# Where attention's first inputs lie, how the relative terms are split, and in what order v and the output's inputs come

## The chip, the cores and the metric

The kernel runs on one core of one Trainium2 chip. The metric is the device time of one launch in microseconds (us); lower is better. The engines are called PE (matrix), DVE (vector), ACT (scalar), POOL and SP; here SP issues nearly all loads, POOL all stores. The chip's 16 DMA engines serve both.

## The reference

x has 48 x 48 = 2304 tokens of 768 channels in float32. Two layers each add a self-attention of the group-normalised x to x:

```python
for layer in (0, 1):
    h = group_norm(x, groups=32)
    q, k, v = split_heads(h @ qkv_w + qkv_b)      # 12 heads of 64; layer 0 adds low-rank terms to q and v
    rel_h = einsum('bhwc,hkc->bhwk', q, Rh)       # 48 values per token
    rel_w = einsum('bhwc,wkc->bhwk', q, Rw)       # 48 values per token
    a = softmax(q * scale @ k.T + rel_h[..., :, None] + rel_w[..., None, :])
    x = x + (a @ v) @ proj_w + proj_b
```

Scores are 2304 x 2304 for each head; rel_h and rel_w add a term by key row and one by key column.

## The kernel before, in words

Tokens are kept in 6 blocks of 384 along the free axis, with channels on partitions (xT). Heads go in 6 pairs of 128 channels. Per layer:

1. **Load and group norm** (L183, L201 on). x is transposed into xT; weights come through `Weights` (L255), which has two pools on the right side of SBUF, one for tables and biases, one double-buffered for weight matrices.
2. **project_kv** (L470). k and v by seven products in place of eight block products (`seven_products`, L425). k is stored to DRAM in a high and a low part (L557). v is computed in 9 iterations, each for two tiles of 128 tokens by 768 channels, and each tile is stored with one DMA from POOL (L584). v tiles alternate between two places.
3. **project_q** (L586). For each half (three pairs of heads) and block: PE makes ps_q (L673), DVE evicts it into x_q (L679), `store` (L613) splits it with `in_parts` (L376 to L386) into a high part, a cast by ACT, and a low part, a subtraction by DVE, in double-buffered part tiles, and stores each from POOL. ACT also copies x_q into `columns` (L684), reordered by image column. The table product psr gives rel_h by block (L632 to L646), straight from PSUM into parts. After the last block of a half, 96 table products psc (L620) in 16 groups of 96 x 432 give rel_w (L648 to L662): copies to a float32 tile relw, by turns on DVE (L658) and ACT (L660), whose writes stride through the tile; then `store` splits and stores relw in six blocks, 12 DMAs of 432 KB for each half.
4. **attend_plain** (L845 on). For a pair of heads and 512 queries, 18 key tiles: `scores` (L931 is the matmul helper) makes a 128 x 1024 score tile in eight matmuls of the q and k parts and two more of the `rel` tile with a 0/1 matrix; ACT takes the exponential (L957); DVE adds it to a sum (L963). `values` multiplies the exponentials with v, a batch of 6 tiles behind the scores. Matmuls are pinned in program order with `in_order` (L158). Inputs come in two sets, by turns: keys (L867, 6 DMAs for a pair), rel (L912, L916, 24 for 512 queries) and q (L902) from SP, v from POOL (L881), 24 DMAs for a pair, which put v's rows into the order of key tiles: a tile has 8 image rows by 16 columns. The two sets are pools on SBUF's left side, set 0 behind a ring of 13 exponential tiles, and set 1 behind it. Set 0's keys are over ground that is early free, its rel, q and v over weight tiles in use until the last ps_q. The output is stored by pair (L1006).
5. **out_project** (L1088). Three pairs of blocks, (0,3), (1,4), (2,5): the attention's output oT (L1082) and the residual (L1118) are loaded by SP, 21 products psy (L1130) a pair, seven for each of three groups of 128 channels, the sum and the next residual stored. `oT` and its helpers lie in left-side pools that start when attention's are free. `begin` (L1163) makes xT and the weights of the next layer; the main loop (L1175 to L1222) calls the stages in turn, and before out_project it issues layer 1's first weights (w_k, L346). `beside` loads the projection matrix (wproj) during attention.

A planner places instructions on each engine by estimated time, except those that `in_order` pins; the engines then run their own lists in order, and synchronise with semaphores. The kernel holds a second version of its attention ("shifted"), for inputs where the exponential could overflow; it is not executed with these inputs.

Of the kernel before, what the change touches and what calls it, by code (L numbers as in the profile page):

```python
# [9 lines left out]
F32 = mybir.dt.float32  # L10
# [8 lines left out]
P = 128  # L19
C = 768  # L20
CT = C // P
# [50 lines left out]
def compute(ctx: ExitStack, tc: tile.TileContext, x, layers, out, run, bad):  # L72
# [182 lines left out]
    class Weights:  # L255
# [7 lines left out]
        def __init__(self, es, ly, li):  # L263
            self.ly, self.li = ly, li
            self.loaded = {}
            self.one = es.enter_context(tc.tile_pool(name="p0_one", bufs=1, side="right", **REUSE))
            self.wp = es.enter_context(tc.tile_pool(name="p0_w", bufs=2, side="right", **REUSE))
            if ly.lora is not None:
                self.ps = es.enter_context(
                    tc.tile_pool(name="ps_f", bufs=2, space=PSUM, **REUSE)  # L270
                )
# [172 lines left out]
    def project(ly, li, xT, kv, weights, first, normalise):  # L444


        PARTS = range(1 if shifted else 2)
        PART = F32 if shifted else F32R
        qd, kd = (
            [[scratch(f"{x}{li}_{half}_{i}", [P, HP, N]) for i in PARTS] for half in range(2)]  # L450
            for x in "qk"
        )
        vd = scratch(f"v{li}", [N, C])
        rel_d = [
            [
                [scratch(f"r{li}_{a}_{half}_{i}", [2 * HG, HP, N]) for i in PARTS]
                for half in range(2)
            ]
            for a in range(2)
        ]  # L460
        project_kv(ly, li, xT, kv, weights, first, normalise, PARTS, PART, kd, vd)
        return qd, kd, vd, rel_d
# [7 lines left out]
    def project_kv(ly, li, xT, kv, weights, first, normalise, PARTS, PART, kd, vd):  # L470


        with ExitStack() as es:
# [28 lines left out]

                return sums, all_steps()

            def multiply(left, right, left_cols, right_cols, transposed, name):
                def product(i):
                    a, b = left[FACTORS[i][0]], right[FACTORS[i][1]]
                    ps = ps_mm.tile([P, QB], F32, tag="mm", name=f"ps_{name}_{i}")
                    for t in range(HP):
                        x, y = a[:, t, left_cols], b[:, t, right_cols]  # L510
                        nc.tensor.matmul(  # L511
                            ps, lhsT=y if transposed else x, rhs=x if transposed else y,
                            start=(t == 0), stop=(t == HP - 1),
                        )
                    return ps

                return product

            everything = slice(None)
            left, steps = first, ()  # L520
            for g in range(3):
                for _ in steps:
                    pass
                for b in range(HB):
# [4 lines left out]
                    def result(at, ps, more):  # L529
# [8 lines left out]
                        nc.vector.tensor_add(to, ps, more)  # L538

                    seven_products(kp, QB, multiply(  # L540
                        left, factors[b], everything, everything, False, f"k_{g}_{b}"
                    ), result)
                    for i in range(2):
                        pair = 2 * g + i
# [22 lines left out]
            for b in range(HB):  # L567
                if b == 1:
                    weights.fold(weights.take("q", 0)[0], 0, 0, ps_mm)
                for j in range(TPB):  # L570

                    place, tag = ((kv, "x"), (vp, "v"))[(b * TPB + j) % 2]
                    v = place.tile([P, 2, C], F32, tag=tag, name=f"v_{b}_{j}")

                    def result(at, ps, more):
                        i, k = int(at[0]) - 1, int(at[1]) - 1
                        nc.vector.tensor_add(v[:, k, ts(i, HP * P)], ps, more)  # L577

                    seven_products(kp, QB, multiply(
                        left, factors[b], everything, ts(j, P), True, f"v_{b}_{j}"  # L580
                    ), result)
                    for k in range(2):
                        at = (b + k * HB) * QB + j * P
                        nc.gpsimd.dma_start(vd[at : at + P, :], v[:, k])  # L584

    def project_q(ly, li, xT, weights, qd, rel_d):  # L586

# [3 lines left out]
        with ExitStack() as es:  # L591
# [55 lines left out]

            def rel_w(half, x):  # L648

                rel = one.tile([P, HP, N], F32, tag="rel", name=f"relw_{half}")[0 : 2 * HG]  # L650
                rel_of = rel.rearrange("p t (h w) -> p w t h", w=HG)
                for l0 in range(0, HG, 3):
                    ps = ps_rel.tile(
                        [2 * HG, 3, HP, HG], F32, tag="rel", name=f"psc_{half}_{l0}"
                    )
                    positions(1, ps, lambda l: x[:, :, l, :], l0, 3)
                    if l0 % 2:
                        nc.vector.tensor_copy(rel_of[:, l0 : l0 + 3], ps)  # L658
                    else:
                        nc.scalar.copy(rel_of[:, l0 : l0 + 3], ps)  # L660
                for b in range(NQB):
                    store(rel_d[1][half], b, rel[:, :, ts(b, QB)], f"relw_{half}_{b}")  # L662

            for half in range(2):
                w, _ = weights.take("q", half)
# [168 lines left out]
    def attend_plain(li, qd, kd, vd, rel_d, od, beside):  # L834
# [10 lines left out]
        ]  # L845
        with ExitStack() as es:

            pp = es.enter_context(tc.tile_pool(name="p2_p", bufs=2 * BATCH + 1, **REUSE))
            sets = [
                es.enter_context(tc.tile_pool(name=f"p2_in{i}", bufs=1, **REUSE)) for i in range(2)  # L850
            ]
            tp = es.enter_context(tc.tile_pool(name="p2_t", bufs=2, **REUSE))
            hp = es.enter_context(tc.tile_pool(name="p2_h", bufs=1, **REUSE))
            ps_s = es.enter_context(tc.tile_pool(name="ps_s", bufs=3, space=PSUM, **REUSE))
            ps_o = es.enter_context(tc.tile_pool(name="ps_o", bufs=1, space=PSUM, **REUSE))

# [16 lines left out]

            def fetch_values(pair):
                v = sets[pair % 2].tile([P, NKT, P], F32, tag="v", name=f"v{li}_{pair}")
                found = vd[:, ts(pair, P)].rearrange(
                    "(b i c w) d -> i w b c d", b=NQB, i=8, w=KG
                )
                for i in range(8):
                    for c in range(TPB):  # L880
                        nc.gpsimd.dma_start(  # L881
                            v.rearrange("p (b c) d -> p b c d", c=TPB)[ts(i, KG), :, c],
                            found[i, :, :, c],
                        )
                return v

            def fetch_queries(i, pair, at, n):
# [197 lines left out]
            )  # L1085
            lo += n

    def out_project(ly, li, od, w, bt, res, xT, next_res, beside):  # L1088


        last = xT is None
        with ExitStack() as es:
            rp = es.enter_context(tc.tile_pool(name="p3_r", bufs=2, **REUSE))
            tp = es.enter_context(tc.tile_pool(name="p3_t", bufs=1, **REUSE))
            kp = es.enter_context(tc.tile_pool(name="p3_k", bufs=2, **REUSE))
            yp = es.enter_context(tc.tile_pool(name="p3_y", bufs=2, **REUSE))
            ps_y = es.enter_context(tc.tile_pool(
                name="ps_y", bufs=4 if last else 8, space=PSUM, **REUSE
# [2 lines left out]
            if last:  # L1101
                op = es.enter_context(tc.tile_pool(name="p3_o", bufs=2 * TPB, **REUSE))
                ps_n = es.enter_context(tc.tile_pool(name="ps_n", bufs=2, space=PSUM, **REUSE))
            for b in range(HB):
                pair = (b, b + HB)
                if last and not shifted and b == HB - 1:
                    judge(ps_n)
                if last:
                    y = yp.tile([P, 2, CT, QB], F32, tag="y", name=f"y_{b}")
                    y = [y[:, i] for i in range(2)]  # L1110
                else:
                    y = [xT[:, i] for i in pair]
                oT = rp.tile([P, 2, CT, QB], F32, tag="oT", name=f"oT_{b}")
                for i in range(2):
                    fetch_output(oT[:, i], od, pair[i])

                for i in range(2):
                    nc.sync.dma_start(y[i], res[pair[i]])  # L1118
                blocks = {
                    f"{i + 1}{j + 1}": oT[:, j, i * HP : (i + 1) * HP]  # L1120
                    for i in range(2) for j in range(2)
                }
                t = tp.tile([P, 4, HP, QB], F32, tag="t", name=f"oT_t_{b}")
# [38 lines left out]
    residuals = [[scratch(f"res{li}_{b}", [P, CT, QB]) for b in range(NQB)] for li in range(2)]  # L1162
    def begin(li, es):  # L1163

        xp, gn = (
            es.enter_context(tc.tile_pool(name=f"{n}{li}", bufs=1, side="right", **REUSE))
            for n in ("x", "gn")
        )
        xT = xp.tile([P, NQB, CT, QB], F32, tag="xT", name=f"xT{li}")
        return xT, gn, Weights(es, layers[li], li)  # L1170

    es = ExitStack()
    xT, gn, weights = begin(0, es)
    for li, ly in enumerate(layers):
# [21 lines left out]
        with tc.tile_pool(name="p3_w", bufs=1, **REUSE) as p3:  # L1196
# [3 lines left out]
            w, steps = sums_of_a(matrix_blocks(w_all, HP * P), *(s[:, i] for i in range(3)))  # L1200

            def beside(w_all=w_all, bt=bt, steps=steps, ly=ly):
                nc.sync.dma_start(w_all, ly.proj_w.rearrange("(t p) n -> p t n", p=P))
                nc.sync.dma_start(bt, ly.proj_bt)
                yield
                yield from steps

            attend(li, qd, kd, vd, rel_d, od, beside())
            es = ExitStack()
            xT = None  # L1210
            if not last:
                xT, gn, weights = begin(1, es)
                weights.begin()
                weights.spread()
                weights.load(0)
                first, k_steps = third_of_k(weights, 0)
            out_project(
                ly, li, od, w, bt, residuals[li], xT,
                None if last else residuals[li + 1], () if last else k_steps,
            )  # L1220
    es.close()


# [53 lines left out]
```

## Time and profile before

| | us |
|---|---|
| median of 3 runs | 3395.48 |
| lowest, highest | 3394.51, 3401.37 |
| profiled execution | 3392.2 |
| its span on the core | 3390.5 |
| PE busy in the span | 3259.3 |
| exponentials L957, 1080 on ACT | 991.3 |

The span is what the hardware profiler saw from the first to the last instruction; the profiled execution's own time has 1.7 us more around it. Lines of groups give the busy time, the mean of one in ns, and after the second bar the engine's idle time just before them with what ended it. Lines of waits give the waiting engine and tile, the releaser, total us, times, longest us. In timelines, the first two numbers are start and length in us. PE's granted clock is given as a share of full speed; it was 0.981 over the span.

### The profile page before, as it was taken

The page shows a single profiled execution, that of the slowest core. Times are in us where ns is not written, and L with a number is a line of the kernel's source. Part 1 is how long each engine was busy: PE and PEld are TensorE (multiplying, and loading weights), DVE is VectorE, ACT ScalarE, POOL GpSimd, SP SyncE. Part 2 cuts the span into 40 slices and gives each one's busy share as a digit, 9 for nine tenths or more (in the row PEclk, how much of TensorE's full clock was granted, in tenths as well). Part 3 has the DMA queues.
Part 4 walks back from the last instruction along what each step waited for, and adds up shares of the span by engine and source line. Part 5 has one row for each costly group of instructions (what it writes and reads, how often), then busy time and mean ns, then how long its engine had stood idle before and what let it go on. Part 6 is the DMA issues. An engine that isn't in the chain of part 4 may idle for free. (4 is left out here: it accounts for less than half of the span.)

```text
span 3390.5 us, 50247 instructions
## 1 busy us (share of the span) xinstructions
PE 3259.3 (96%) x19708; PEld 2005.6 (59%) x19708; DVE 2111.9 (62%) x2267; ACT 1425.6 (42%) x1647; POOL 439.5 (13%) x795
## 2 busy tenths in 40 slices
PE   8999987999999999998989999699999999999997
PEld 5556664565656565655555566556565656566554
DVE  8533446777777676776674234467777677777753
ACT  3101445555555555552011024455555555555511
POOL 2101222020202020000011012400101020100000
PEclk9999998999999999999999999899999999999998
DMA  7322477353626262524233146654445352624051
GB/s 257 135 79 96 152 230 204 77 126 76 136 67 145 59 153 59 108 62 165 84 140 130 65 138 225 187 133 96 116 90 121 81 129 74 137 67 103 28 200 57
DMA packets 200723, 405.61 MB, mean 120 GB/s; under 512 B 42608, under 2 KB 82448, under 8 KB 197408
## 3 DMA queue, kind: packets, MB, share of 16 engines
q1 hardware_dynamic: 150816, 238.84, 28.7%
q0 software_dynamic: 49664, 163.47, 14.3%
q8 instruction: 159, 2.61, 0.3%
q14 instruction: 84, 0.69, 0.1%
HBM read 253.27 MB, written 148.89 MB: 119 GB/s over the span
## 5 line engine op out<-in xcount | busy, mean ns | idle before, releaser
L957 ACT ACTIVATE pt<-ps_sc 128x1024 f32<-128x1024 f32 (+1 forms) x1080 | 991.3, 939 | 663.1 <-PE ps_sc L931 595.8
L963 DVE TENSOR_TENSOR sum<-sum,pt 128x1024 f32<-128x1024 f32 (+1 forms) x960 | 1072.7, 1117 | 314.4 <-ACT pt L957 230.4
L931 PE MATMUL ps_sc<-q,k 64*128 64x512 f32 (+1 forms) x8640 | 1099.6, 374 | 59.0 <-ACT pt L957 58.4
L931 PEld LDWEIGHTS ps_sc<-q,k 64*128 64x128 f32 x8640 | 774.3, 186 | 326.8 <-issue 92.2
L931 PE MATMUL ps_ov<-pt,v 128*64 128x512 f32 (+1 forms) x4320 | 884.3, 554 | 0.0
L931 PEld LDWEIGHTS ps_ov<-pt,v 128*64 128x64 f32 x4320 | 293.5, 137 | 474.8 <-issue 432.9
L931 PE MATMUL ps_sc<-rel,places 64*128 64x512 f32 (+1 forms) x2160 | 410.9, 371 | 0.0
L673 PE MATMUL ps_q<-xT,w_q 128*128 128x384 f32 x864 | 285.8, 489 | 0.7 <-DVE v L577 0.7
L1008 POOL DMA_DIRECT2D f_rec<-rec x120 | 58.8, 495 | 1658.3 <-DVE rec L997 1609.5
L997 DVE RECIPROCAL rec<-ps_d 128x512 f32<-128x512 f32 (+1 forms) x60 | 182.2, 3037 | 100.7 <-PE ps_d L931 100.7
L673 PEld LDWEIGHTS ps_q<-xT,w_q 128*128 128x128 f32 x864 | 163.7, 192 | 111.2 <-issue 2.3
L931 PEld LDWEIGHTS ps_sc<-rel,places 64*128 64x128 f32 x2160 | 210.4, 185 | 29.7
L881 POOL DMA_DIRECT2D v<-f_v x288 | 148.7, 527 | 171.3 <-PE ps_ov L931 144.0
L511 PE MATMUL ps_k<-xt,w_k 128*128 128x384 f32 x432 | 143.4, 487 | 3.6 <-DVE xt L420 2.6
L679 DVE TENSOR_SCALAR x_q<-ps_q,bt 128x384 f32<-128x384 f32 x72 | 44.4, 616 | 137.5 <-PE ps_q L673 133.2
L511 PE MATMUL ps_k<-xT,w_k 128*128 128x384 f32 x324 | 115.6, 510 | 4.7 <-DVE xT L248 4.6
L511 PEld LDWEIGHTS ps_k<-xt,w_k 128*128 128x128 f32 x432 | 81.5, 190 | 63.0 <-PE ps_k L511 3.0
L972 ACT CAST sum<-sum 128x1024 bf16<-128x1024 f32 (+1 forms) x60 | 57.6, 961 | 129.0 <-DVE sum L963 129.0
L973 DVE TENSOR_TENSOR sum<-sum,sum 128x1024 f32<-128x1024 f32 (+1 forms) x60 | 67.1, 1119 | 61.6 <-ACT sum L972 61.6
L975 DVE TENSOR_TENSOR sum<-sum,sum 128x1024 bf16<-128x1024 f32 (+1 forms) x60 | 67.1, 1119 | 61.6 <-ACT sum L974 61.6
L381 ACT ACTIVATE xs_q<-x_q 128x1152 fp32r<-128x1152 f32 x24 | 27.9, 1164 | 181.1 <-DVE x_q L679 175.7
L963 DVE TENSOR_TENSOR sum<-pt 128x1024 f32<-128x1024 f32 (+1 forms) x60 | 67.1, 1118 | 56.9 <-ACT pt L957 55.8
(167 smaller groups left out, 2468.1 us busy)
## 6 DMA issues: line engine op xcount, KB each, us to landing
rel<-f_r SPq DMA_DIRECT2D x1152, 96.0 KB, 4.1
f_k<-xs POOLq DMA_DIRECT2D x72, 384.0 KB, 2.9
k<-f_k SPq DMA_DIRECT2D x72, 384.0 KB, 5.6
f_q<-xs_q POOLq DMA_DIRECT2D x48, 576.0 KB, 3.8
q<-f_q SPq DMA_DIRECT2D x96, 256.0 KB, 3.0
f_r<-relh POOLq DMA_DIRECT2D x48, 432.0 KB, 5.0
f_r<-relw POOLq DMA_DIRECT2D x48, 432.0 KB, 6.0
f_v<-v POOLq DMA_DIRECT2D x36, 384.0 KB, 2.6
```

The lines of the kernel that those rows point to most:

```text
L511: nc.tensor.matmul(ps, lhsT=y if transposed else x, rhs=x if transposed else y, start=(t == 0), stop=(t == HP - 1),)
L673: nc.tensor.matmul(ps, lhsT=w[:, t, ts(pr, P)], rhs=xT[:, b, t, :], start=(t == 0), stop=(t == CT - 1),)
L679: nc.vector.tensor_scalar(x[:, pr], ps, weights.bt[:, pair : pair + 1], ly.q_scale, ALU.add, ALU.mult,)
L881: nc.gpsimd.dma_start(v.rearrange("p (b c) d -> p b c d", c=TPB)[ts(i, KG), :, c], found[i, :, :, c],)
L931: in_order(nc.tensor.matmul(*args, **kwargs))
L957: nc.scalar.activation(pt, ps[:, :, 0 : self.n], AF.Exp)
L963: nc.vector.tensor_add(self.sum, self.first if kt == 1 else self.sum, pt)
L972: nc.scalar.copy(hi, self.sum)
L973: nc.vector.tensor_sub(self.sum, self.sum, hi)
L975: nc.vector.tensor_sub(lo, self.sum, mid)
L997: nc.vector.reciprocal(self.rec, ps)
L1008: nc.gpsimd.dma_start(recs[li][2 * self.pair + r : 2 * self.pair + r + 1, to], self.rec[r * HD : r * HD + 1, :],)
```

## The change

- **Rel terms.** `rel_w` no longer copies psc to a float32 tile. Each group goes with `in_parts` straight into two part tiles of the whole half: ACT casts the high part, DVE subtracts it from PSUM, both with the same strided writes. Each part is stored with one DMA for the half.
- **v's order.** Each v tile is stored with 16 DMAs of 16 rows, to the rows of DRAM where key tiles have them, and `fetch_values` is one DMA from SP for a pair.
- **Pools.** On the right side, the tables' pool is now outermost, then x, then the group norm's, then the weights' (a new method `room`). On the left, attention's pools are in the order set 1, rec and o, sum, exponential ring, set 0. The addresses of the built program show set 0 over what was xT (161,024 to 216,320 bytes of a partition), and v of set 0 partly over the tables; so keys and rel of set 0 wait for the last ps_q, and v for the last psc. Set 1 lies over the part tiles.
- **out_project.** The order of the pairs is (1,4), (0,3), (2,5). The first pair's oT goes into two blocks of the new xT (layer 0), or into a new pool on the right side (layer 1, also its residual); w_k of layer 1 is loaded after the first pair's loads. The projection matrix's two loads are pinned in program order.
- `multiply` is rewritten and gives the same matmuls.

```diff
@@ Weights
             self.one = es.enter_context(tc.tile_pool(name="p0_one", bufs=1, side="right", **REUSE))
+
+        def room(self, es):
             self.wp = es.enter_context(tc.tile_pool(name="p0_w", bufs=2, side="right", **REUSE))
@@ project_kv
                     for k in range(2):
-                        at = (b + k * HB) * QB + j * P
-                        nc.gpsimd.dma_start(vd[at : at + P, :], v[:, k])
+                        at = (b + k * HB) * QB
...
+                        for r in range(P // KG):
+                            i, c = divmod(8 * j + r, TPB)
+                            to = at + c * P + i * KG
+                            nc.gpsimd.dma_start(vd[to : to + KG, :], v[ts(r, KG), k])
@@ project_q, rel_w
-                rel = one.tile([P, HP, N], F32, tag="rel", name=f"relw_{half}")[0 : 2 * HG]
-                rel_of = rel.rearrange("p t (h w) -> p w t h", w=HG)
+                parts = [
+                    one.tile([P, HP, N], PART, tag=f"rel{i}", name=f"relw_{half}_{i}")[0 : 2 * HG]
+                    for i in PARTS
+                ]
                 for l0 in range(0, HG, 3):
...
-                    if l0 % 2:
-                        nc.vector.tensor_copy(rel_of[:, l0 : l0 + 3], ps)
+                    to = [
+                        r.rearrange("p t (h w) -> p w t h", w=HG)[:, l0 : l0 + 3] for r in parts
+                    ]
...
-                        nc.scalar.copy(rel_of[:, l0 : l0 + 3], ps)
-                for b in range(NQB):
-                    store(rel_d[1][half], b, rel[:, :, ts(b, QB)], f"relw_{half}_{b}")
+                        in_parts(*to, ps)
+                for found, part in zip(rel_d[1][half], parts):
+                    nc.gpsimd.dma_start(found, part.bitcast(F32))
@@ attend_plain
-            pp = es.enter_context(tc.tile_pool(name="p2_p", bufs=2 * BATCH + 1, **REUSE))
-            sets = [
-                es.enter_context(tc.tile_pool(name=f"p2_in{i}", bufs=1, **REUSE)) for i in range(2)
-            ]
-            tp = es.enter_context(tc.tile_pool(name="p2_t", bufs=2, **REUSE))
-            hp = es.enter_context(tc.tile_pool(name="p2_h", bufs=1, **REUSE))
+            in1, tp, hp, pp, in0 = (
+                es.enter_context(tc.tile_pool(name=f"p2_{name}", bufs=bufs, **REUSE))
+                for name, bufs in (
+                    ("in1", 1), ("t", 2), ("h", 1), ("p", 2 * BATCH + 1), ("in0", 1)
+                )
+            )
+            sets = [in0, in1]
...
-                found = vd[:, ts(pair, P)].rearrange(
-                    "(b i c w) d -> i w b c d", b=NQB, i=8, w=KG
-                )
-                for i in range(8):
-                    for c in range(TPB):
-                        nc.gpsimd.dma_start(
-                            v.rearrange("p (b c) d -> p b c d", c=TPB)[ts(i, KG), :, c],
-                            found[i, :, :, c],
-                        )
+                nc.sync.dma_start(v, vd[:, ts(pair, P)].rearrange("(t p) d -> p t d", p=P))
@@ out_project
-            for b in range(HB):
+            for at, b in enumerate((1, 0, 2)):
...
+                if at == 0:
+                    oT = first[:2]
                 else:
-                    y = [xT[:, i] for i in pair]
-                oT = rp.tile([P, 2, CT, QB], F32, tag="oT", name=f"oT_{b}")
+                    oT = rp.tile([P, 2, CT, QB], F32, tag="oT", name=f"oT_{b}")
+                    oT = [oT[:, i] for i in range(2)]
...
+                if at == 0:
+                    next(beside, None)
@@ main loop
-                nc.sync.dma_start(w_all, ly.proj_w.rearrange("(t p) n -> p t n", p=P))
+                in_order(nc.sync.dma_start(w_all, ly.proj_w.rearrange("(t p) n -> p t n", p=P)))
...
+            if last:
+                p3_first = es.enter_context(
+                    tc.tile_pool(name="p3_first", bufs=1, side="right", **REUSE)
+                )
...
             else:
                 xT, gn, weights = begin(1, es)
+                first_out = [xT[:, HB - 1], xT[:, NQB - 1]]
...
+            def prepare(weights=weights):
                 weights.load(0)
-                first, k_steps = third_of_k(weights, 0)
+                prepared.extend(third_of_k(weights, 0))
+                yield
+                yield from prepared[1]
```

## The prediction

> **What bounds the kernel now.** I read the page's first sections, then what TensorE (PE) waits for, then tables by stage, then the timeline of the two places where PE stands still.
>
> ```profile
> PE 3259.3 (96%) x19708; PEld 2005.6 (59%) x19708; DVE 2111.9 (62%) x2267; ACT 1425.6 (42%) x1647; POOL 439.5 (13%) x795
> ```
> ```profile
> PE ps_sc L931 <- ACT pt L957: 58.4, 42, 22.8
> PE psy L1130 <- DMA oT<-f_o: 11.8, 2, 8.7
> ...
> PE psc L620 <- DVE relh L385: 5.6, 4, 2.2
> ...
> PE psr L620 <- DVE relh L385: 4.1, 1, 4.1
> ```
> PE is busy 3259.3 of 3390.5 us, so an edit that leaves the matmuls alone can win only from 131 us of gaps. Half of that is in two rows: 58.4 us for the softmax's exponentials (L957), longest 22.8, and 11.8 us for out_project's first loads.
>
> ```profile
> 490.00:500.00 10.00, 10.00 (x84) 9.12 (x82) 5.80 (x7) 6.63 (x7) 2.22 (x4) 1.00 1.05 263
> 500.00:510.00 10.00, 0.22 (x2) 0.00 (x0) 3.27 (x4) 2.30 (x2) 3.79 (x6) 0.73 1.03 346
> 510.00:520.00 10.00, 0.00 (x0) 0.00 (x0) 3.05 (x3) 2.30 (x2) 2.57 (x5) 0.50 0.98 316
> 520.00:530.00 10.00, 4.49 (x20) 3.11 (x22) 2.44 (x3) 5.16 (x5) 7.03 (x14) 0.50 0.94 257
> ```
> Columns: stretch, length, busy us of PE, its loader, DVE, ACT, POOL; granted clock, DMA share, GB/s. At layer 0's attention PE stands still for 20 us; DVE and ACT are mostly idle and the DMA engines full. ACT's instruction order explains it:
>
> ```profile
> L660 ACT COPY relw<-psc 96x432 f32<-96x432 f32 x32 | 28.4, 888 | 22.1 <-PE psc L620 22.1
> L384 ACT CAST relw<-relw 96x1152 fp32r<-96x1152 f32 x24 | 27.3, 1152 | 47.3 <-DMA f_r<-relw 38.5 <-DVE x_q L679 3.5 <-DVE relw L658 2.5
> L385 DVE TENSOR_TENSOR relw<-relw,relw 96x1152 fp32r<-96x1152 f32 x24 | 32.2, 1353 | 45.2 <-DMA f_r<-relw 38.6 <-ACT relw L384 6.5
> L385 DVE TENSOR_TENSOR relh<-psr,relh 96x432 fp32r<-96x432 f32 x48 | 28.3, 602 | 27.7 <-ACT relh L384 15.7 <-DMA f_r<-relh 5.8 <-DMA f_r<-relw 4.7
> L384 ACT CAST relh<-psr 96x432 fp32r<-96x432 f32 x48 | 23.9, 514 | 34.5 <-PE psr L620 13.2 <-ACT columns L684 8.3 <-DMA f_r<-relh 5.8
> ```
> The six splits of relw (L384, L385) stand ahead of the first exponential; they use double-buffered parts, so each waits until an earlier store has left (38.5 us). The stall is a DMA wait shown as "ACT". PE's own timeline brackets it, and shows the second place:
>
> ```profile
> 484.55 12.00 PE L620 MATMUL psc<-columns,tab 128*96 128x144 f32 x96 [2.17 <-DVE relh L385]
> 496.48 1.20 PE L931 MATMUL ps_sc<-q,k 64*128 64x512 f32 x8
> ```
> ```profile
> 1575.34 6.36 PE L1130 MATMUL psy<-oT,wproj 128*128 128x384 f32 x12 [8.67 <-DMA oT<-f_o]
> ```
>
> [...] the strided relw copy takes 0.888 us, the contiguous relh cast of the same 96x432 0.514. [...] Here, in 500–520, loads got about 28%: 1.85 of 6.6 MB, the rest 11 relw stores.
>
> **Part 1: relw straight into two parts.** Gone per half: 16 copies and 12 splits. New: 16 ACT copies (0.89) and 16 DVE subtractions at price s, then two stores of 2.65 MB (96 rows x 6912 values) in place of twelve of 432 KB, so 40 fewer DMAs on POOL in all. For s: below, 0.88, one strided side as in the copy; above, 1.65, if the relh row's 0.60 is charged for a strided read and a strided write, 0.5 each, as ACT's strided columns copy (2.19 against 1.16 contiguous) and the relw copy suggest. I take 0.95[...]. Nothing below 0.88: the output is written with the copy's stride.
>
> Each psc group's PSUM buffer (three, L608 of the new kernel) is held for 0.74 on PE, 0.89 on ACT, 0.95 on DVE and three handovers of 0.24 (timeline): 3.3 us, so a group leaves every 1.10 us. The 16th may start after the 13th's subtraction: 12 x 1.10 + 3.3, plus its own 0.74, is 17.2 against 12.0. So each of four psc phases costs PE 5 us; nothing else is there to hide it.
>
> At the attention starts what is behind is freed: the last copy ends near 484.55 + 18.3, the table load (1.28) and the first exponential follow, and PE's three tiles (1.15 each) just cover that. The seventh score tile starts at 484.55 + 17.2 + 6 x 1.15 + 0.6 = 509.2; before, 532.25: 23 us. In layer 1, 2145.61 + 17.2 + 1.7 (lower clock) + 7.5 = 2172.0 against 2194.12: 22 us. Together 45, the psc loss inside.
>
> Half 0 to half 1: layer 0 loses 5. Layer 1 loses 5 but the 4.1 us psr wait (third table) goes, with 1.7 of slow matmuls beside it, since the rel loads that met the stores come later. Net loss 4. Half 0's two large stores cost nothing while the projection (some 70 us) covers them; uncovered, 5.3 MB at 330 GB/s (the mean of 500–520) is 16 us.
>
> **Part 2: first inputs where x was.** keys, rel and q now wait for the last ps_q, 479.5 (only q and some rel did in layer 0; in layer 1 keys and rel had been there by 2106). SP has 6.4 MB to bring with v (DMA issues: keys 6 x 384 KB, rel 24 x 96, q 2 x 256, v 24 x 48). In 480–500 the engines moved 5.5 MB, 2.0 of it stores of q and relh, so 3.5 are in by 500, 0.9 more by 503. The last 2.0 (rel's end, then v, now one load behind them on SP) meet 5.3 MB of stores. An even share of 330 GB/s lands v at 515, 28% at 525. It is needed 6.9 us after the seventh tile, 516. Queued behind it on PE are the first values' matmuls and all later scores. Stall 0 to 9 per layer; I take 3.5, 7 together.
>
> **Part 3: v in key-tile order.** 36 stores become 288 of 16 rows, 288 loads become 12 on SP. POOL's price hardly depends on size (0.495 for one row, 0.542 for 128x768), so 16 x 0.53 = 8.5 us per iteration of 13.54 us; a v tile has two buffers, so its stores have a second iteration to land, and the next POOL work after the last iteration (298.1) is q's store at 312.3. The planner writes some v sums later on DVE, behind k's, which PE does not wait for; the products' helper is rewritten and gives the same matmuls. Zero, between 0 and what R3 gives. The 149 us of POOL loads removed were hidden: only their first set was near the path.
>
> **Part 4: out_project.** Its first block pair is now (1, 4), as old as (0, 3) by then. Its first loads go into places free earlier: layer 0, 1564.3 (eighth of the last twelve value tiles) instead of 1566.17, and w_k comes after them rather than ahead; 2.36 MB at 379 GB/s plus latency lands about 1572, so 3 us of the 8.67 go, with 2.3 of a later wait (product 5 came 8.1 after the first; 5.8 unstalled). Layer 1's are free before attention ends: 3.12 and 1.8 go. Sum 10.5, between 7 and 13; the projection weights' order costs nothing under attention.
>
> **Sum.** −45 + 7 + 4 − 10.5 = −44.5; 3392.2 − 44.5 = 3347.7. The profiled execution is 3.3 below the median, 3395.48, so 3351.
>
> **Rivals.** R1: the subtraction adds up, s = 1.65, and DVE paces psc: 13 x 1.65 + 3.0 = 24.5 per phase, 7.5 worse four times, 7 of v's stall regained: 3374. For it: no row shows both strides free. [...]
> R2: loads lose to the stores, as before the change (28%): 9 to 12 us of stall per layer, at 12 17 worse: 3368. Against: POOL's packets were as large then.
> R3, slower: POOL becomes the bound of the v phases, 18 iterations, (16p − 13.54) x 18. It decides from p = 0.85; slower than before from p = 1.0. At p = 1.1, 73 us: 3424. For it: eight outstanding stores must land in 8p; against: 384 KB landed in 2.6 us.
> R4: the exponential has a wait that I don't see, and both attention stalls stay: psc costs 4 x 5, out_project gives 10.5, the psr wait 5.8; 3399, no change within 0.2%. Against: the new program has no split ahead of the exponential.
>
> **Chances.** Forecast 0.50, R1 0.22, R2 0.20, R3 0.04, R4 0.04. With s = 0.88 and no stall the time is near 3341; 1 in 10 stays below or just at that. The range 3332 to 3378 takes in R1 and R2. A measurement tells 0.2% (6.8 us) from no change: faster 0.92, same 0.04, slower 0.04.
>
> **What would show it.** Right: the 22.8 us wait gone, subtractions near 0.95, psc phases of 17 us, v landing by 520, psy's wait in layer 1 gone. Wrong: subtractions over 1.3 (R1), ps_ov or ps_sc waiting for DMA of v or k over 8 us (R2), ps_v waiting behind POOL (R3).

## The result, and the profile after

The changed kernel takes 3376.3 us (median of 4 runs, 3374.5 to 3377.3) against 3396.7 in the same session: ratio 0.9938, 95% interval 0.992 to 0.9955. That is 20 us faster, where 44.5 were forecast; the time lies near the slow end of the forecast's range (3332 to 3378). The profiled execution took 3375.6 us, with a span of 3373.9, 16.6 us below the span before.

The page's first section and the waits of PE, as for the kernel before:

```profile
PE 3263.2 (97%) x19708; PEld 2003.5 (59%) x19708; DVE 2104.7 (62%) x2275; ACT 1426.5 (42%) x1655; POOL 387.3 (11%) x719
```
```profile
PE ps_ov L944 <- DMA v<-f_v: 31.5, 2, 17.1
...
PE ps_sc L944 <- ACT pt L970: 8.1, 36, 0.2
...
PE psy L1151 <- DMA xT<-f_o: 4.3, 1, 4.3
...
PE ps_d L944 <- ACT sum L985: 2.5, 1, 2.5
```
The 58.4 us for the exponentials are 8.1, none longer than 0.2; the psr wait is gone; psy waits 4.3 instead of 11.8. But the first row is new: PE waits for v at the start of both attentions, 17.1 and 14.4 us. The last row is new too. The same stretch of layer 0 as before the change:

```profile
500.00:510.00 10.00, 9.48 (x76) 7.79 (x78) 6.87 (x9) 9.10 (x10) 1.04 (x2) 1.00 1.04 299
510.00:520.00 10.00, 8.16 (x72) 6.57 (x68) 9.27 (x8) 8.38 (x9) 0.00 (x0) 1.00 1.02 332
520.00:530.00 10.00, 0.00 (x0) 0.00 (x0) 2.75 (x3) 0.00 (x0) 0.00 (x0) 0.57 0.68 201
530.00:540.00 10.00, 4.72 (x16) 1.57 (x18) 0.00 (x0) 0.00 (x0) 0.00 (x0) 0.58 0.57 159
```
Work goes on in 500 to 518 and then stops, with the DMA engines at 0.68 and 0.57, no longer full. Who waits for what is in the timelines of PE, POOL and SP (start, length, engine, operation):

```profile
535.28 6.90 PE L944 MATMUL ps_ov<-pt,v 128*64 128x512 f32 x24 [17.11 <-DMA v<-f_v]
```
```profile
505.43 0.52 POOL L680 DMA_DIRECT2D f_r<-relw  x1 [15.26 <-ACT relw L387]
506.46 0.51 POOL L680 DMA_DIRECT2D f_r<-relw  x1 [0.50 <-DVE relw L388]
```
```profile
507.25 2.44 SPq L897 DMA_DIRECT2D v<-f_v  x1
```
The load of v is issued 2 us after the first store of relw and lands 28.0 us later. Layer 1 does the same: issued at 2153.5, landed at 2180.9.

What the two DMA queues moved meanwhile (q0 is POOL's, with the stores; q1 is SP's, with the loads; packets, megabytes, share of the engines' time), first in the kernel before, 500 to 520, then in the changed one, from v's issue to 520:

```profile
q0 software_dynamic: 1076, 4.28, 67.3%
q1 hardware_dynamic: 1281, 2.34, 33.0%
```
```profile
q0 software_dynamic: 162, 4.06, 99.1%
q1 hardware_dynamic: 118, 0.14, 3.1%
```
The loads' share of the bytes falls from 35% to 3%.

The new instructions cost what was forecast:

```profile
L388 DVE TENSOR_TENSOR relw<-psc,relw 96x432 fp32r<-96x432 f32 x64 | 56.1, 924 | 12.0 <-ACT relw L387 11.8
L387 ACT CAST relw<-psc 96x432 fp32r<-96x432 f32 x64 | 54.7, 907 | 12.7 <-PE psc L633 12.4
L597 POOL DMA_DIRECT2D f_v<-v x288 | 137.9, 488 | 105.3 <-DVE v L583 94.0 <-issue 11.2
```

Where the time went, measured between the same events in both timelines, in us:

| stretch | forecast | measured |
|---|---|---|
| psc of half 0, two layers | +10 | +7.1 |
| layer 1's psr wait and its slow matmuls | −5.8 | −6.0 |
| psc start to first value matmul of half 1, layer 0 | −23 + 3.5 | −7.8 |
| the same, layer 1 | −22 + 3.5 | −9.6 |
| first to last value matmul, layer 0 | 0 | +1.1 |
| the same, layer 1 | 0 | +7.0 |
| last value matmuls to first psy, layers 0 and 1 | −3, −3.1 | −4.4, −2.7 |
| first psy to product 5, layers 0 and 1 | −2.3, −1.8 | 0, −0.7 |

The measured rows sum to −16.0 of the span's −16.6; the rest is spread over the other stages.

### The profile page after: what moved, and what is told of

It is laid out like the page before. It is cut to its first block, busy times and chain, and to the rows that moved or that the text cites. A ratio compares the mean times of both kernels' runs of the same rounds, so it can differ in the third digit from the quotient of the medians.

```text
span 3373.9 us, 50053 instructions
## 1 busy us (share of the span) xinstructions
PE 3263.2 (97%) x19708; PEld 2003.5 (59%) x19708; DVE 2104.7 (62%) x2275; ACT 1426.5 (42%) x1655; POOL 387.3 (11%) x719
## 5 line engine op out<-in xcount | busy, mean ns | idle before, releaser
L944 PE MATMUL ps_ov<-pt,v 128*64 128x512 f32 (+1 forms) x4320 | 889.3, 556 | 31.5 <-DMA v<-f_v 31.5
L597 POOL DMA_DIRECT2D f_v<-v x288 | 137.9, 488 | 105.3 <-DVE v L583 94.0
```

The lines of the kernel that those rows point to most:

```text
L597: nc.gpsimd.dma_start(vd[to : to + KG, :], v[ts(r, KG), k])
L944: in_order(nc.tensor.matmul(*args, **kwargs))
```

## The experiments

My theories after the result. A: v starves behind relw's stores, because their pieces are so much larger than its own, 27,648 bytes against 512. B: one DMA of 2304 pieces of 512 bytes takes 28 us in any case. Later A was split: A2, the pieces decide: where both queues have work, they advance about piece for piece, as in the kernel before in 500 to 520, 927 of the stores' to 1034 of the loads' (a piece is what the trace records as one packet); A3, the stores simply have to leave first.

Totals alone mislead here: in the profiled executions the time between the last output store's issue and the end of the span is about 19 us for some kernels and 7 to 9 for others (last section). So the table has both, from the profiled execution of each kernel; the median is of all its runs, the ratio against runs of the kernel before in the same session.

| kernel | median | ratio to before (95%) | last store issued | time behind it |
|---|---|---|---|---|
| before | 3396.7 | | 3371.3 | 19.2 |
| changed | 3376.3 | 0.9938 (0.992–0.9955) | 3354.7 | 19.2 |
| v_early | 3357.2 | 0.9882 (0.9865–0.9898) | 3338.9 | 19.1 |
| small_rows | 3365.2 | 0.9898 (0.9874–0.9922) | 3355.8 | 7.0 |
| no_store | 3352.0 | 0.9869 (0.9853–0.9886) | 3327.6 | 18.9 |
| judge_whole | 3372.4 | 0.9926 (0.9909–0.9942) | 3352.5 | 19.2 |
| v_long | 3356.2 | 0.988 (0.9853–0.9906) | 3341.4 | 7.0 |
| v_long_small | 3341.7 | 0.9829 (0.981–0.9848) | 3330.9 | 7.7 |
| early_small | 3333.8 | 0.9804 (0.9788–0.9821) | 3324.8 | 7.1 |
| parts_alone | 3394.2 | 0.9988 (0.9982–0.9995) | 3383.2 | 8.6 |
| early_judge | 3326.4 | 0.9803 (0.9786–0.9819) | 3314.4 | 7.0 |
| early_judge_long | 3330.3 | 0.9811 (0.9794–0.9827) | 3320.2 | 7.9 |
| psc_five (one run) | 3372.0 | | 3351.2 | 19.1 |
| no_out | 3383.1 | 0.9964 (0.9952–0.9977) | 3363.1 | 19.1 |

Two cautions. In small_rows, v_long, v_long_small, early_small and both early_judge kernels POOL pauses before the end and issues its last three or four stores together, so the last store is a late mark there. PE's last matmul ends at 3369.6 in the kernel before, 3353.0 in the changed one, 3351.9 in small_rows, 3320.9 in early_small and 3310.5 in early_judge. And v_long's four runs lie at 3349.8, 3350.2, 3362.2 and 3367.0, small_rows' between 3353.3 and 3367.6: the medians of these two are rough, and what follows rests on waits and landings.

### v_early: v asked for before the stores

```diff
-            keys, queries = fetched(fetch_keys(0), fetch_queries(0, *blocks[0]))
-            v = fetch_values(0)
+            found = (fetch_keys(0), fetch_queries(0, *blocks[0]))
+            for g in range(NG):
+                if g == NG - 1:
+                    v = fetch_values(0)
+                for _, step in found:
+                    step(g)
```
Layer 0's low-rank tile is also allocated before the tables, which puts them beyond v's ground.

> The changed kernel, with v of the first set loaded by SP ahead of the last third of keys and rel instead of behind it, and layer 0's tables moved off v's ground, so that v is asked for some 5 us before relw's two stores. Theory A (v starves behind the stores: their rows of 27,648 bytes hold a DMA engine 1.4 us each, v's pieces of 512 bytes 28 ns): v lands 7 to 12 us after its issue, the 17.1 and 14.4 us waits fall to under 3 each, and the time to 3340 to 3350; some of it may come back as a wait for the second block's q and rel, which need the first store to have landed. Theory B (one DMA of 2304 pieces of 512 bytes takes its 28 us in any case): v lands near 528, waits of 10 us stay, the time is near 3365.

v was issued at 500.9, 3.9 us before the first store, and landed 6.6 us later (6.5 in layer 1):

```profile
DMA to landing us min/median/max: 6.6/6.6/6.6
```
B falls: the same DMA, in the same form, takes a quarter of the time when nothing is ahead of it. All of v's waiting is gone, and a part comes back on the loads that are now last:

```profile
PE ps_sc L945 <- DMA rel<-f_r: 9.1, 2, 6.9
...
PE ps_sc L945 <- issue: 2.9, 1, 2.9
```
That is the last third of rel of the first set, not the second block's q and rel that I had named; hence 3357 and not 3350.

### small_rows: the same stores, in twelve DMAs

```diff
-                for found, part in zip(rel_d[1][half], parts):
-                    nc.gpsimd.dma_start(found, part.bitcast(F32))
+                for b in range(NQB):
+                    for found, part in zip(rel_d[1][half], parts):
+                        nc.gpsimd.dma_start(
+                            found[:, :, ts(b, QB)], part[:, :, ts(b, QB)].bitcast(F32)
+                        )
```


> The changed kernel, with each half's two relw stores cut by query block into twelve, of 96 rows by 3 x 384 values, which are the pieces of the kernel before; bytes, engine and time of issue are the same. Theory A with its point that the size of the rows starves v: v gets a share from its issue on, lands by 518 to 526 instead of 535, waits 0 to 8 us a layer, time 3352 to 3366. If only the bytes ahead matter (5.3 MB have to leave first), or v's own form (theory B): v lands at 533 to 537 and the time stays at 3376 within 4 us.

```profile
PE ps_ov L947 <- DMA v<-f_v: 28.7, 2, 14.4
```
v's waits are 14.4 and 14.2, against 17.1 and 14.4. So cutting the stores' pieces to a sixth is not enough: A as first stated is refuted, or incomplete. The total seems to say otherwise (11 us less), but PE's last matmul ends only 1.1 us earlier than in the changed kernel; nearly the whole gain lies behind it. The expectation has one thing wrong: the time of issue is not the same. POOL waits for earlier stores to land and issues the last three in layer 0 between 513 and 520, where the changed kernel has issued both by 507.

### v_long and v_long_small: v in long pieces

```diff
-        vd = scratch(f"v{li}", [N, C])
+        vd = scratch(f"v{li}", [N, C] if shifted else [CT, P, NKT, P])
...
-                            to = at + c * P + i * KG
-                            nc.gpsimd.dma_start(vd[to : to + KG, :], v[ts(r, KG), k])
+                            nc.gpsimd.dma_start(
+                                vd[:, ts(i, KG), at // P + c, :].rearrange("g p d -> p g d"),
+                                v[ts(r, KG), k].rearrange("p (g d) -> p g d", d=P),
+                            )
...
-                nc.sync.dma_start(v, vd[:, ts(pair, P)].rearrange("(t p) d -> p t d", p=P))
+                nc.sync.dma_start(v, vd[pair])
```


> The changed kernel, with v kept in DRAM by pair of heads, then by row of a key tile, then by tile, so that one partition's v of a pair is one piece of 9216 bytes instead of 18 of 512. Place and time of the load, and the two large stores of relw, stay. Theory A2 ([...] cutting the stores alone did not help, because 512 bytes against 4608 is still a tenth): [...] v lands some 15 us after its issue, at 520 to 525, waits 2 to 7 us per layer, time 3348 to 3362. Theory A3 (v has to wait until the stores have left whatever its pieces are): v lands at 530 or later, 3370 or more.

> As v_long, and the stores of relw cut into twelve of pieces of 4608 bytes as in small_rows. Theory A2: v's pieces are now the longer, [...] lands about 6 to 9 us after its issue, at 514 to 517, no wait is left, and the time is 3336 to 3350. Theory A3: v lands at 528 or later and the time is that of small_rows, near 3365.

small_rows and v_long_small differ only in how v lies in DRAM, and so in the pieces of its load, 512 against 9216 bytes (and in the runs that v's own stores write, long before). In layer 0 v was issued at 507.5 and 509.4; the first value matmul came at 532.4, after a wait of 14.4, against 519.9 without one. In layer 1 the wait is 14.2 against 0.9, the one that v_long_small has left:

```profile
PE ps_ov L949 <- DMA v<-f_v: 0.9, 1, 0.9
```
The stores are the same. In v_long_small's layer 0 the last piece of v moved at 519.4 while pieces of the stores went on to 532.1; in small_rows v's pieces went on to 531.9 and the stores' to 530.5. So A3 falls for this pair, and A2 fits.

v_long, with the large stores left, is mixed: in layer 1 v landed in 10.0 us and nothing waits, in layer 0 in 24.5 us with a wait of 16.5. In layer 1 v was issued 0.1 us before the first store, and its pieces moved from 2156.9 to 2163.4, the stores' first only at 2160.1: that is order again. In layer 0 v was issued 4.7 us after the first store, behind loads of rel on its own queue, and its first piece moved at 523.7; from 511 to 523 the queue moved 117 of rel's pieces of 2048 bytes beside 145 of the stores'. So v's long pieces had little chance to show their worth there.

The trace's records of single packets show how the two queues advanced. Counted without the packets of 4 bytes:

| kernel and stretch (us) | stores' pieces, bytes | loads' pieces, bytes |
|---|---|---|
| before, 500 to 520 | 927 of 4608 | 814 of 2048, 220 of 3072 |
| changed, 508 to 513 | 54 of 27,648 | 7 of 2048 |
| changed, 515 to 520 | 57 of 27,648 | 34 of 512, 22 of 2048 |
| changed, layer 1, 2158 to 2168 | 121 of 27,648 | 129 of 512 |
| small_rows, 511 to 517 | 224 of 4608 | 1180 of 512, 4 of 2048 |
| small_rows, 519 to 524 | 337 of 4608 | 415 of 512 |
| v_long_small, 513 to 517 | 98 of 4608 | 105 of 9216, 3 of 2048 |

In five of the seven stretches the two queues move about one piece for one. In the changed kernel, 515 to 520, a store's piece takes 1.37 us and a load's 27 ns (512 bytes) or 84 ns (2048), so nearly all of the time goes to the stores. The other two stretches show that this isn't the whole story: just after the stores start, the loads get far less, and in small_rows, around POOL's pauses, far more. The records don't say which of the 16 engines moved a packet, so why stays open. Layer 0's 28 us in the changed kernel also have a part that isn't v's own: its first piece moved at 515.1, behind the last of rel on the same queue.

### early_small: both

> v_early with the stores cut as in small_rows. v lands at 508 as in v_early. In v_early PE waits 9.1 us in one layer and 5.1 in the other for rel of the first set, whose pieces of 2048 bytes meet pieces of 27,648. [...] rel now meets pieces of 4608 bytes, [...] and is in time: waits under 3 us in sum, time 3343 to 3352. If the stores have to leave first (A3), the waits stay, 3357.

A2 is the theory that gives 3343 to 3352. v landed in 7.7 and 6.6 us. The waits for rel:

```profile
PE ps_sc L948 <- DMA rel<-f_r: 1.7, 2, 0.9
```
From 12.0 (9.1 and the 2.9 beside it; 6.9 of them in layer 0, where the expectation has 9.1) to 1.7, by the stores' pieces alone. So the size of the stores' pieces does count for loads of 2048 bytes, as A2 says, and was not enough for those of 512. The last store is issued at 3324.8, 29.9 us before that of the changed kernel; PE's last matmul ends 32.1 us earlier.

### no_store: nothing stored at attention's start

```diff
-                for found, part in zip(rel_d[1][half], parts):
-                    nc.gpsimd.dma_start(found, part.bitcast(F32))
+                elif half == 0:
+                    for to in rel_d[1]:
+                        for found, part in zip(to, parts):
+                            nc.gpsimd.dma_start(found, part.bitcast(F32))
```


> Leaves out the stores of the second half's relw: the first half's parts are stored twice in their place, so heads 7 to 12 get the first half's column term and the output is another. It shows the time when nothing is stored at attention's start. Theory A: v lands about 8 us after its issue, at 515 to 516, no wait for it is left, the second set is loaded at once, and the time is 3338 to 3346. Theory B: v still lands after 528 and 20 us of waits stay.

This kernel leaves out the stores of the second half's relw. No wait for v, keys or rel is left: what held v were the stores. The time, 3352, is above my 3338 to 3346, since the doubled stores of half 0 are not as free as I took them: PE waits 5.1 us for x_q, and psc of half 1 ends 7 us later in layer 0.

```profile
PE ps_q L696 <- DVE x_q L702: 5.1, 2, 3.0
```

### judge_whole: the check of the reciprocals in one pass

This is about the last row of the waits after. The kernel ends by testing that the softmax's reciprocals lie in a safe range. The planner had moved the first half of this test up on DVE, ahead of the last block's sums. In the changed kernel (timeline of DVE and PE):

```profile
3208.11 0.27 DVE L1076 TENSOR_SCALAR low<-judged 128x216 f32<-128x216 f32 x1 [3.75 <-DMA judged<-f_rec]
...
3208.73 3.08 DVE L976 TENSOR_TENSOR sum<-sum,pt 128x512 f32<-128x512 f32 x4
...
3211.84 0.62 ACT L985 CAST sum<-sum 128x512 bf16<-128x512 f32 x1 [6.04 <-DVE sum L976]
...
3212.51 0.30 PE L944 MATMUL ps_d<-sum,ones_k 128*64 128x256 bf16 x2 [2.51 <-ACT sum L985]
```
```diff
-                nc.vector.tensor_scalar(low[:, li, :], r[:, li, :], REC_MIN, None, ALU.is_ge)
-                nc.vector.scalar_tensor_tensor(
-                    r[:, li, :], r[:, li, :], REC_MAX, low[:, li, :], ALU.is_le, ALU.mult,
-                    accum_out=good[:, li : li + 1],
-                )
+            nc.vector.tensor_scalar(low, r, REC_MIN, None, ALU.is_ge)
+            nc.vector.scalar_tensor_tensor(
+                r, r, REC_MAX, low, ALU.is_le, ALU.mult, accum_out=good[:, 0:1],
+            )
```


> The changed kernel, with the check of the reciprocals done in one pass over both layers' values (one comparison and one product of 432 columns instead of two each of 216), so that it can't start before the last block has finished. If the 4.0 us that PE waits for ACT's sums in layer 1's last block come from DVE waiting 3.75 us for the first of the two loads, both waits go and the time falls by 3 to 5 us, to 3372. If DVE is late there for another reason, PE's wait stays and the time is the same within 1 us.

The waits of ps_d are gone, and the time is 4 us lower, 3372.4, although v's waits are 2.1 us longer in its profile (33.6). Four of the 7.0 us lost inside layer 1's attention are this. The other three are the slow clock behind the stall: the first 24 value matmuls take 8.37 us there and 5.37 in the next batch; PE's granted clock was 0.50 from 2170 to 2185 and 0.80 in the 5 us after. So are layer 0's 1.1 (6.90 for the first 24).

### parts_alone: the kernel before with the rel terms alone

Its edit is the diff of `rel_w` shown with the change, in the kernel before.

> The kernel before with one part of the change, rel_w straight into two parts with two stores for each half; v's order, pools and out_project as before. The exponentials' ring and the first keys then lie over the new parts, so the first exponential waits for relw's stores to land, some 17 to 20 us after psc, instead of for six splits. Expected: four psc phases 3.6 us longer each, the psr wait of layer 1 gone (6 us), a first stall of 15 to 22 us per layer as before: 3390 to 3410. If the splits alone held ACT up and the stores don't matter, the stall goes and the time falls below 3370.

```profile
PE ps_sc L936 <- ACT pt L962: 45.6, 41, 14.3
```
ACT's first exponential now waits 16.2 us for relw's stores to land, because the ring lies over the parts. The stalls of attention's start stay. The median is 0.1% below before, but the last store is issued 11.9 us later and the time behind it is 10.6 us shorter. So up to the last store the part alone loses; it needs the pools' new places.

### psc_five, no_out: two terms by themselves

```diff
-            ps_rel = es.enter_context(tc.tile_pool(name="ps_rel", bufs=3, space=PSUM, **REUSE))
+            ps_rel = es.enter_context(tc.tile_pool(
+                name="ps_rel", bufs=3 if ly.lora is not None or shifted else 5, space=PSUM, **REUSE
+            ))
```


> The changed kernel, with five instead of three PSUM buffers for the table products in layer 1, where the banks are free; layer 0 keeps three. If the chain of PE, ACT and DVE through three buffers sets the pace of psc (0.977 us a group), layer 1's groups come at the pace of ACT or DVE, some 0.95, and PE, running two groups further ahead, starts the scores 2 to 3 us earlier than with three, while layer 0 stays. If DVE's subtraction alone sets the pace, the groups' pace stays at 0.97 to 0.98 and only the two groups ahead, up to 2 us, are won.

With five buffers PE goes through layer 1's 16 groups in 11.98 and 12.07 us, without a wait for DVE, against 15.4 before the next ps_q and 16.5 before the first score with three. DVE's 16 subtractions run back to back in 13.41 us, 0.838 each. So with three buffers the chain through PSUM set the pace; and I had underrated what two more buffers let PE run ahead (4.4 us in layer 1, 2 to 3 expected). Little of it is in the total, since v's waits grow to 36.5.

no_out takes the out_project part out of the changed kernel: its edit puts back the order (0,3), (1,4), (2,5), left-side tiles for all inputs and w_k's load ahead of them.

> The changed kernel without its part for out_project: pairs in the order (0,3), (1,4), (2,5), their inputs on the left side, w_k ahead of them. By the traces of the changed kernel the part is worth 4.4 us in layer 0 and, since DVE's early check takes back 4 us, less than nothing in layer 1: 3377 to 3381. If it is worth the 10.5 us of the prediction, 3385 to 3388.

It lost 8.5 us by its last store, and 0.26% by the ratios. My expectation from the table above was too low: without the part, psy waits 10.7 us in layer 0, longer than before the change, and 3.0 us for DVE's oT_t in layer 1, which the kernel before did not show.

```profile
PE psy L1144 <- DMA oT<-f_o: 10.7, 1, 10.7
...
PE psy L1144 <- DVE oT_t L423: 3.0, 1, 3.0
```

### early_judge and early_judge_long: what beats both kernels

> early_small with the check of the reciprocals in one pass as in judge_whole. If the two waits are independent, the last output store is issued 3 to 5 us before that of early_small (3324.8), near 3321. The stretch behind that store was 19.2 us in some kernels and 7.1 us in others, and I know no rule for it: 3330 with the short one, 3342 with the long one.

> early_judge with v's longer pieces as in v_long. v is already in time there, so longer pieces should gain nothing at attention's start; the stores of v have more and shorter pieces. Last output store within 2 us of early_judge's, 3319 to 3323; if v's later loads had still cost something, up to 5 us earlier.

early_judge takes 3326.4 us, 0.9803 of before. Its list of waits has no line for ps_d or for DMA of v or rel; the largest is for x's first load. PE's last matmul ends 42.6 us before that of the changed kernel; the 10 us that are saved behind it I can't claim for any of the edits. Single profiles differ by some 3 us before any edit acts (psc of half 1 in layer 0 starts at 486.6 here and at 490.2 in early_small), so the 10.4 us to early_small are not all the check. The longer pieces on top gain nothing, as expected; the 5.8 us lost are outside the 2 us I had given. 3 us of them are a wait for ps_k between the layers (3.57, 0.70 without). v_long_small has the same 3.57 and v_long 0.69; its cause stays open.

## Why the prediction was wrong, point by point

**What bounded the kernel, and part 1: right, with one thing left out.** The exponential's wait went: from psc's start, the seventh score tile starts 25.0 us earlier in layer 0 and 24.0 in layer 1, where 23 and 22 were forecast. The subtraction took 0.924 us (0.95 forecast) and 0.838 without waits, below the floor of 0.88 that I had set. So two strided sides do not add up here: the copy with one takes 0.890. R1 is out. My 0.95 was an estimate: no row of the kernel before has both sides strided, and why they don't add up, no run shows. A psc phase lost 3.6 us in half 0 (5 forecast), 3.7 and 2.9 before the scores. The reason given, three PSUM buffers, was confirmed by psc_five. parts_alone shows what the forecast left out: with the splits gone and the pools where they were, ACT's first exponential waits 16.2 us for the stores instead. The gain needs the pools too.

**Part 2 failed: "An even share of 330 GB/s lands v at 515, 28% at 525", "stall 0 to 9 per layer; I take 3.5".** The stall was 17.1 and 14.4, and 4 us more through the clock. I shared the engines by bytes, from a share seen with loads of 2048 and 3072 bytes against pieces of 4608. Even that share was misread: the loads moved 2.34 of 6.62 MB, 35% and not 28%, and by pieces it was 1034 to 927. The change made the stores' pieces six times as large, 27,648 bytes in place of 4608. And it took v's load from POOL's queue, where the trace has it in packets of 3072 bytes (six runs of 512), to SP's, where each run of 512 is a packet (2304 for layer 0's first pair). Packets of 3072 for v beside the large stores were not run. At about one packet for one, the loads' share of the bytes fell to 3%. So R2's "POOL's packets were as large then" was wrong. R2 had the right direction, and 9 to 12 us a layer for it. v_early, small_rows against v_long_small, and no_store leave no other holder of v than relw's stores. This term alone is worth some 24 of the 28 us by which the span missed the forecast (2 x 3.5 taken, 31.5 measured); the sum has smaller ones on both sides.

That the two queues would share the bytes evenly was my estimate, and equal numbers of unequal pieces are no equal shares. The counts show about equal numbers in five of the seven stretches, as in 121 to 129; 54 to 7 just after the stores' start is not even that.

**Half 0 to half 1: right** in layer 1's psr wait, 6.0 against 5.8. **Part 3: right.** A store costs POOL 0.488 us, 16 of them 7.8 of 13.54 us; R3 did not come. Its eight outstanding DMAs show in the kernel before: four of POOL's loads of v, issued at 488.63, 490.74, 492.40 and 494.42, each came 0.2 to 0.3 us after the landing of the DMA that POOL had issued eight before. In the changed kernel v's stores land in 2.0 us (median), and eight issues take 3.9. (These are 8 for each of an iteration's two v tiles; the description of the change says 16 for each, which is wrong.) **R4 did not come.**

**Part 4: the start right, the size too large.** 4.4 and 2.7 us came where I had 3 and 3.1. The other 4.1 (product 5) was no DMA wait: in layer 0 product 5 starts 8.1 us after the first psy in both kernels, and no wait lies between them. The first 12 matmuls alone take 6.4 us, against 4.03 for 12 later ones: PE's granted clock was 0.58 from 1565 to 1570 and 0.74 in the 5 us after. And I missed that inputs that come early let the planner move the check, 4.0 us. In the changed kernel the part is worth 8.5 us all the same (no_out). Two sums in the prediction are slightly off: this part's four terms add up to 10.2, not 10.5, and R1's phase is 7.2 us longer, not 7.5.

**What would have shown it:** the two entries of the list, "v landing by 520" and "waiting for DMA of v … over 8 us (R2)", were the right ones; v landed at 535, and PE waited 17.1 us.

## What to carry to other kernels

When a store is made larger, ask which small loads share the DMA engines with it: count pieces and how long each takes (here 1.37 us for 27,648 bytes, 27 ns for 512), not bytes. Here order helped most: the load that was issued 3.9 us before the stores landed in 6.6 us, the one issued 2 us after the first of them in 28.0. And a stall that is freed at one end is worth only the time until the next input; write down when each of the next inputs lands, with its piece size, before taking the whole gap as gain.

## What the runs showed of the hardware that I had not expected

- Where both queues had work, they often advanced about piece for piece whatever the sizes: 121 stores' pieces of 27,648 bytes beside 129 of v's of 512 in 10 us. It is no fixed rule: 54 to 7 in the 5 us after the stores' start.
- DVE's subtraction with PSUM input, strided second input and strided output takes 0.838 to 0.924 us for 96 x 432, as much as the strided copy with one strided side (0.890).
- Behind the last output store, POOL's closing drain takes 10.28 us and the semaphore step ahead of it 2.68 in before, the changed kernel, v_early, judge_whole, psc_five and no_out (10.11 and 2.64 in no_store), but 0.89 to 0.97 and 0.4 in small_rows, v_long, v_long_small, early_small and both early_judge kernels, and 1.86 and 0.63 in parts_alone. It is alike in the profiles of before and after, so the comparison of these two is free of it, but it moves other totals: from PE's last matmul to the end it is 20.6 to 20.9 us in the first group and 10.3 to 11.6 in the others. Each kernel has one profiled execution, and v_long's runs (3350, 3350, 3362, 3367) are as far apart as the two groups, so it may change from run to run; what decides it stays open.
